# Queries in two halves of 50, 128-column score weights, and a planner that counts ScalarE's table: one change to a four-layer cross-attention kernel

## The chip, the cores and the metric

The kernel runs on one core of one Trainium2 chip. TensorE (PE for its matmuls, PEld for its weight loads), VectorE (DVE), ScalarE (ACT), GpSimd (POOL) and SyncE (SP, which issues the DMAs) run side by side, each through its own list of instructions, in that list's order; they wait for one another on semaphores. The metric is device time in microseconds of one launch; lower is better.

## The reference

The input is a batch of 16 with 100 query rows of 256 numbers (`x`), and a context of 361 rows of 256 numbers (`ctx_1024`) with a mask over the 361 keys. Everything is fp32. Four cross-attention layers follow each other, each with 16 heads:

```
L0: LayerNorm(x), LayerNorm(ctx); Q,K,V with biases, head size 16; softmax(QK^T/4) V; Wo, residual;
    LayerNorm, w1 (256 -> 1024), exact GELU, w2 (1024 -> 256), residual
L1: RMSNorm(x); Q,K,V without biases, head size 64; softmax(QK^T) V; Wo, residual
L2: Q,K,V, head size 64; rotary embedding of Q and K; mask; softmax(QK^T/8) V; Wo, residual; LayerNorm
L3: LayerNorm(x), LayerNorm(ctx); Q,K,V with biases, head size 16; softmax(QK^T/4) V; Wo, residual
```

So for each of the 16 batch elements and each layer there are 16 score matrices of 100 x 361, which need a softmax, a transposition (TensorE contracts over partitions), and a product with V.

## The kernel before

**Work list and planner.** `tile_xattn_layers` does not issue instructions as it goes. Each step (`Plan.add`) is recorded as a piece of work: the engines that may do it with its estimated occupancy and latency in ns, the buffers it reads and writes, and, for TensorE, the array's mode. `Plan.order` then takes pieces one at a time: it looks at all whose inputs are done and whose buffers are free, estimates when each could start on its best engine, and takes the earliest. Ties go by rank. A rank is the batch's place times `ORDER["lag"]`, less the length of the chain of work behind the piece, plus a number of its own out of the long list `ORDER["place"]`. The result is one fixed list for each engine. Two batch elements are under way at a time, in buffers of parity `p = b % 2`, so that one's column work lies beside the other's softmax.

**TensorE's modes.** The 128 x 128 array is used in parts. `on_columns` (line 726) cuts the weights into 32 columns and runs four matmuls beside each other (mode `col32`; the projections, the products with V, the output projections and the feed-forward). Scores of head size 64 (line 832) and all transpositions run as two halves of 64 rows each (`row64`); scores of head size 16 run as four quarters of 32 rows (`row32`). The planner adds `Plan.CHANGE[mode]` when it goes from one mode to another, and `ORDER["keep"]`, `"run"` and `"pull"` hold it in a mode or draw it to one.

**One unit of attention** (`Attention.unit`, 4 heads; 4 units a layer, 256 in all): `scores` writes four PSUM banks, one a head, with the queries as weights (100 columns) and the keys moving in two parts of 181 and 180 columns. For each head `exponential` copies the scores out of PSUM negated with their maximum (DVE, line 885; with the mask lines 879 and 882) and takes the exponential with its sum on ACT (line 891). For each pair of heads `softmax` inverts the sums (DVE, line 855) and divides (POOL, line 862). `transposed` (line 926) turns the 100 x 384 probabilities into 3 x 128 x 100: a transposition loads 128 columns of probabilities as weights and moves the identity. The rows are cut at 64, so the two that run beside each other have 64 and 36 rows, and move 64 and 36 columns. Each pair's first 64 queries go to one PSUM bank and are copied to `pT` (384 columns); the last 36 of both pairs share a bank `rest`, copied once a unit (432 columns). `copied` (lines 607 ACT, 609 DVE) lets the planner choose the engine. `weighted` multiplies by V (line 726).

**Around it.** `inv_root` and `normalize` (lines 632 and 643, POOL) make the norms, `queries_T` (line 667) transposes normalized queries, and its copies are lines 607 and 609, or 687 and 689 where a scale and a shift go with it. `keys_T` (754) transposes the context, `rows_of` (709) transposes back. `rotated` (781 to 793) applies the rotary embedding. `feed_forward` computes GELU in 8 ACT instructions (line 1257). Exponential and GELU are in different tables of ScalarE, so the program has a table load ahead of the first exponential after a GELU and ahead of each GELU block. The planner before has that load only in the estimate of the GELU piece (`8 * 245.0 + 2560`); the load itself stands in the program where the next exponential is.

**Start.** SP's queue issues the context, `x`, the column vectors `crow`, and the weight slabs in that order. The second context transfer waits for a memset of `ctxr` on POOL.

Of the kernel before, what the change touches and what calls it, by code (L numbers as in the profile page):

```python
# [26 lines left out]
SCORE_BANKS = 5  # L27

# [3 lines left out]
for _name, _w in (  # L32
# [23 lines left out]
    "lag": 262500, "pull": 1.05, "window": 0,  # L56
    "keep": {None: 4710, "row64": 360, "row32": 180, "col64": 5940, "col32": 2180},
    "run": {None: 0, "row64": 28190, "row32": 38220, "col64": 62800, "col32": 390},
    "batch": (-548000, -33500, 0, 0, 0, 0, 0, 0, 0, 0, 0, 0, 0, 0, 14000, -395500),
    "place": [  # L60
        100 * k for k in (
        1776, 1453, -142, -1201, -1962, -875, -1272, -1989, 482, -1959, -1129, -88, -4927,
        -3879, -2673, -19, -2982, 335, 200, -5963, -3867, -2489, -3290, -3547, -1559, -3672,
        602, 1581, -1237, -596, -892, -2024, -2482, -2746, -3675, -6084, -4418, -2962, -2419,
        -2347, -1399, -1767, -676, -4804, -3312, -4682, -3996, -950, -4319, -2634, 152, -4596,
        -4245, -4636, -3397, -2411, -4617, -1436, 1812, 478, -590, -3084, -3225, -157, -347,
        -1306, -36, -182, 2463, 2269, 2471, -1236, -226, -48, -2453, -824, -689, -240, -1480,
        -391, -171, 371, -1768, -2183, -2349, -2481, 1673, -1111, 32, 25, 1577, -514, -23,
        -1722, 3615, 62, -2886, -1417, -3429, -5371, -2487, -917, 340, -2084, 948, 1034, -1280,
        376, -1062, -727, 190, -606, 1116, -1324, -1597, -131, -943, 1382, 2231, 2480, -3400,  # L70
        -748, -2254, -1153, -2683, -2519, -1789, -5353, -2696, -2986, -2331, -2031, -4065,
        -3099, -2421, -171, -2559, 1016, -6786, -2846, -2199, -1555, -157, -1767, -1656, -3138,
        -1222, 2168, -631, -524, -4580, -574, 597, -514, -1139, 1487, 1898, -982, -233, 477,
        2044, -522, -2119, -3681, -1016, -671, 2120, 3576, 2286, -266, 3381, 723, 247, 1826,
        774, 948, -3623, -2236, 984, -2841, 310, 61, 2466, -3684, -6034, 1564, 1183, -2853, 537,
        -1192, -2567, -1296, 108, -3693, 149, -718, -1842, 780, 685, 1596, 3206, 156, 3888,
        1907, 2379, 1212, 1530, -3100, 2948, 1039, -288, -1177, -1310, -2820, -3017, 433, 151,
        -39, 1813, -33, 2599, -2329, -1178, -1118, 1344, -1750, -3151, -1387, -3185, -3845,
        -8129, -7410, -4599, -3978, -4283, -3026, -4766, -6536, -4866, -4851, -8579, -4112,
        -6439, -1860, -481, -2093, -540, -2396, -4045, -1076, -2195, -70, 1766, 165, -176,  # L80
        -1338, -918, -12, 1834, 2889, 1336, -1772, 1062, -3022, 2129, 611, 1207, -2448, -6678,
        -981, -133, 380, -1319, -722, -558, 2201, 2070, 640, 1748, 2253, 4103, 5971, 5712, 4011,
        3044, 722, 5181, 4108, 5603, 2863, 3615, 4070, 3505, 4100, 1973, 2673, 3145, 3356, 3367,
        5844, 3350, 2666, 6351, 2740, 5441, 3794, 495, 3120, 2070, -601, -856, -2641, 335,
        -2107, -3659, -1701, 378, 778, 1172, -739, 1007, 542, -108, -2248, 2953, -1482, -932,
        3100, -1364, 1555, 3374, 238, 3536, 4315, 3827, 4485, 3600, 2067, -880, 4682, 3885,
        3987, 5494, 4942, 6102, 3437, 4869, 1221, 3493, 1237, 2378, 1389, 266, 2904, 2874, 2176,
        936, -826, -1283, -1678, 654, -2718, -7, 4162, -524, -774, 511, -684, 3038, -1031, 2912,
        3195, 2452, 575, 493, 2016, 1582, 1498, -1241, -2078, -1407, -3506, -2378, -1649, -3375,
        -3472, -878, -594, -94, -2271, -2722, -2086, -5299, -6556, -4953, -2896, -463, -5380,  # L90
        -2620, -2181, -2583, -1142, 273, -2589, -3385, 987, 2285, 484, 765, -386, 3057, 1070,
        1200, 292, 763, 26, -5488, -2236, 259, -6763, -2594, -4453, -4645, -7113, -8246, -5633,
        -8943, -5849, -8851, -9101, -6157, -3672, -4940, -4203, -6547, -7698, -5075, -2078,
        -1789, -4219, -2670, -227, 100, 3388, 4070, 1516, -104, 2126, -432, 2456, 2021, 4097,
        2055, 2009, 6506, -667, -54, -1179, -34, 3966, 2359, -414, 1217, 3474, 2676, -1197, 857,
        1108, 4961, 1038, -3603, -260, 94, -1383, -960, 4578, 3569, 4863, 3041, 4067, 3943, 559,
        629, 1048, -963, 504, 79, -56, 734, 1352, 375, 1930, -2827, 1022, -297, 1587, 3516,
        -1027, -845, 1898, -1616, -1197, 384, 2016, 3496, 4418, 2467, 2775, 3097, 3600, 2898,
        3321, 435, -99, -1056, 4084, 2305, 1957, 2885, 1769, 3160, 1712, -4221, -1615, -1270,
        708, 999, -245, 44, 3282, 2595, 5822, 2335, 3929, 2251, 3141, -1056, -1690, -851, 1712,  # L100
        -289, 1963, 4576, 4722, 1801, -432, 1256, -1161, 1210, -3366, -1607, -3406, -2015, 1592,
        -266, -2447, -512, -1015, -345, -469, -4154,
# [19 lines left out]
class Work:  # L122
    __slots__ = (
        "engines", "fn", "bufs", "takes", "next", "then", "n_after", "ready", "tail", "batch",
        "mode", "modes", "index", "start", "end", "engine", "place", "rank",
# [25 lines left out]
class Plan:  # L151

    CHANGE = {"row64": 170, "row32": 191, "col32": 141, None: 190}
# [18 lines left out]
    def add(self, engines, fn, reads=(), writes=(), takes=(), mode=None, begun=()):  # L172
# [3 lines left out]
        w.engines, w.fn, w.batch = engines, fn, self.batch  # L176
# [36 lines left out]
    def order(self):  # L213
# [11 lines left out]
        mode, run = None, 0.0  # L225
# [5 lines left out]
        while len(done) < len(self.work):  # L231
            held, able, at_hand = set(), [], {}
            for _, i in ready:
# [23 lines left out]
                for e, occ, lat in w.engines:  # L257
                    s = max(t, free_at[e])
                    if e == "PE" and not set_now:
                        lat = lat + self.CHANGE[w.modes[0]]  # L260
                    if cost is None or s + lat < cost - 1:
                        engine, cost, start, busy = e, s + lat, s, occ
# [15 lines left out]
            if e == "PE":  # L278
                run = run + occ if set_now else occ
                if not set_now:  # L280
                    mode = w.modes[0]
                    occ += self.CHANGE[mode]
                w.mode = mode
            else:
                w.mode = e
            free_at[e] = start + occ
# [24 lines left out]
def tile_xattn_layers(  # L311
# [18 lines left out]
    def slots_of(name, n, shape, dtype=F32, pool=const):  # L330
# [16 lines left out]
        "two": slots_of("two", 32, [P, 2]),  # L347
        "mv": slots_of("mv", 8, [P, NKC, 8]),
    }
    for p in range(2):  # L350
# [5 lines left out]
        slots[f"qT{p}"] = slots_of(f"qT{p}", 1, [P, 8, S])  # L356
# [11 lines left out]
    for t in slots["prob"]:  # L368
        nc.gpsimd.memset(t[:S, SK:], 0.0)
# [71 lines left out]
    crow = const.tile([NCOLS, P], F32, name="crow")  # L441
# [5 lines left out]
    crow_b = load_const(crow, colvecs, 0.1, "crow")  # L447
# [26 lines left out]

    colt = const.tile([P, NCOLS], F32, name="colt")
# [3 lines left out]
    def transpose_cols(_):  # L479
        nc.tensor.transpose(cps.ap[:, :NCOLS], crow, ident[:NCOLS, :NCOLS])  # L480
# [4 lines left out]
    plan.add(on_pe((NCOLS, 1)), transpose_cols, reads=[crow_b], writes=[cps])  # L485
# [155 lines left out]
    def normalize(mv, dst, src, dst_f, src_f, j, n):  # L641
# [6 lines left out]
        plan.add(on_pool(395), fn, reads=[mv, src], writes=[dst])  # L648
# [121 lines left out]
    def rotated(ps, n, cos, sin, dst, dst_f, rep, rot, name):  # L770
# [3 lines left out]
        def shaped(a):  # L774
            return a.rearrange("p (r s) -> p r s", r=rep) if rep > 1 else a

        def wide(a):
            return a.unsqueeze(1).to_broadcast([P, rep, n // rep]) if rep > 1 else a
# [4 lines left out]
        def times_sin(_):  # L783
            a = shaped(sw.ap[:, :n])
            nc.gpsimd.tensor_tensor(a, a, wide(sin()), ALU.mult)  # L785

        def times_cos(_):
            nc.vector.tensor_tensor(
                shaped(dst_f(dst.ap)), shaped(ps.ap[:, :n]), wide(cos()), ALU.mult
            )  # L790

        def both(_):
            nc.gpsimd.tensor_tensor(dst_f(dst.ap), dst_f(dst.ap), sw.ap[:, :n], ALU.add)  # L793
# [6 lines left out]
    class Attention:  # L800
# [17 lines left out]
        def unit(self, i):  # L818
# [9 lines left out]
            def scores(_):  # L828
                for g in groups:
                    for k0, k1 in ((0, half), (half, SK)):  # L830
                        for h in g:
                            nc.tensor.matmul(  # L832
                                banks[h].ap[:S, k0:k1], lhsT=self.q_of(h),
# [15 lines left out]
        def softmax(self, banks, shares, pair, name, probs):  # L849
            sums, rsum = (plan.buf("two", f"{k}_{name}") for k in ("sum", "rsum"))  # L850
            for j, h in enumerate(pair):
                self.exponential(banks[h], shares[h], sums, j, h, probs)

            def inverse(_):
                nc.vector.reciprocal(rsum.ap[:S], sums.ap[:S])  # L855

            plan.add(on_dve(2), inverse, reads=[sums], writes=[rsum])
            for j, h in enumerate(pair):
                p = probs[h]

                def divide(_, j=j, p=p):
                    nc.gpsimd.tensor_scalar(  # L862
                        p.ap[:S, :SK], p.ap[:S, :SK], rsum.ap[:S, j : j + 1], 1.0,
# [5 lines left out]
        def exponential(self, bank, share, sums, j, h, probs):  # L869

            neg_max = plan.buf("two", f"mx_{self.name}_{h}")
            prob = probs[h] = plan.buf("prob", f"prob_{self.name}_{h}")
            masked = self.cap is not None

            def p():
                return prob.ap[:S, :SK]
# [516 lines left out]
```

## Time and profile before

| | |
|---|---|
| Time, median of 3 runs | 1972.56 us (1968.7 to 1972.88) |
| The profiled execution | 1968.26 us, of which the span is 1966.5 us |
| Granted TensorE clock, mean | 0.995 |
| Busy: PE / PEld | 1924.7 us / 1269.7 us |
| Busy: DVE / ACT / POOL | 1276.4 us / 1196.7 us / 1042.4 us |
| Transpositions of probabilities, line 926 | 6144 loads, 6144 matmuls |
| Scores, line 832 | 4096 loads, 4096 matmuls (two for each in the program) |
| Copies to `pT` | 540 on ACT, 228 on DVE |
| Table loads on ACT | 33, of 1283 ns each |

A group's mean is the time from dispatch to the modelled end of one instruction, and matmuls overlap, so the pace of TensorE is not read from means but from when instructions of a run start. A line such as `1028.18 0.58 PE L926 MATMUL ... x12` in the timeline says that 12 matmuls of line 926 began at 1028.18 us and the last ended 0.58 us later; `[0.59 <-POOL prob L862]` says that the engine sat idle for 0.59 us and what ended that. In the list of waits the three numbers are the total in us, how often, and the longest.

### The profile page before, as it was taken

The numbers are of one execution on the slowest core, as the hardware profiler recorded it, in microseconds if no ns is written. First come the engines' busy times: TensorE is split into PE (matmuls) and PEld (weight loads), VectorE is DVE, ScalarE is ACT, GpSimd is POOL, SyncE is SP. The second block draws the span as 40 slices with busy tenths as digits, with TensorE's granted clock in tenths as the row PEclk, the third lists the DMA queues.
The fourth block names the chain that finished last, engine by engine and source line by source line (L and its number), as shares of the span: only waits on it lengthen the run. The fifth ranks groups of instructions, "written<-read, shape, count | busy, mean of one in ns | idle before, by whom it ended". The sixth has DMA issues, their size and how long they took to land.

```text
span 1966.5 us, 99772 instructions
## 1 busy us (share of the span) xinstructions
PE 1924.7 (98%) x43881; PEld 1269.7 (65%) x43881; DVE 1276.4 (65%) x4452; ACT 1196.7 (61%) x3470; POOL 1042.4 (53%) x1680
## 2 busy tenths in 40 slices
PE   8999999999999999999999999999999999999997
PEld 4667666666666666666666666666656666665666
DVE  4556667766576665766657676566766657765576
ACT  4656656665566656666556565665666556665546
POOL 5354645545455564655546555464654545554464
PEclk9999999999999999999999999999999999999998
DMA  7000000000000000000000000000000000000000
GB/s 300 3 3 14 5 12 8 3 14 5 12 7 3 14 6 14 5 5 12 5 14 6 11 8 3 14 5 12 7 3 14 5 12 8 3 14 5 3 3 7
DMA packets 14731, 29.95 MB, mean 15 GB/s; under 512 B 3362, under 2 KB 12376, under 8 KB 12888
## 3 DMA queue, kind: packets, MB, share of 16 engines
q1 hardware_dynamic: 14296, 23.56, 3.8%
q8 instruction: 345, 5.65, 1.2%
q14 instruction: 90, 0.74, 0.1%
HBM read 21.92 MB, written 1.64 MB: 12 GB/s over the span
## 4 chain that ended last, share of the span: by engine, by line
PE 89%; POOL 3%; ACT 3%; DVE 2%; issue 1%; DMA 1%; SPq 0%; DVEq 0%; POOLq 0%; ACTq 0%
PE ps L726 64%; PE ps L832 14%; PE ps L926 10%; ACT prob L891 1%; POOL prob L862 1%; DVE prob L885 1%; PE ps L667 1%; ACT L891 1%; DVE pT L609 1%; POOL kT L793 1%; POOL sw L785 0%; DMA slab<-slabs_dram 0%; PE ps L754 0%; DMA mask<-mask_dram 0%; PE ps L709 0%
## 5 line engine op out<-in xcount | busy, mean ns | idle before, releaser
L862 POOL TENSOR_SCALAR prob<-prob,two 100x361 f32<-100x361 f32 x1024 | 568.2, 570 | 478.1 <-DVE two L855 390.1
L891 ACT ACTIVATE prob<-prob,two 100x361 f32<-100x361 f32 x1024 | 604.8, 595 | 141.1 <-DVE prob L885 101.4
L885 DVE TENSOR_SCALAR_CACHE_REDUCE prob<-ps 100x361 f32<-100x361 f32 x768 | 375.1, 528 | 79.2 <-PE ps L832 61.5
L726 PE MATMUL ps<-slab,cT 128*32 128x512 f32 (+1 forms) x3072 | 360.8, 595 | 0.0
L726 PE MATMUL ps<-cT,slab 128*32 128x361 f32 x4096 | 348.1, 469 | 2.5 <-DVE prob L885 1.8
L832 PE MATMUL ps<-kT,qT 32*100 32x181 f32 (+3 forms) x4096 | 301.1, 327 | 0.4 <-ACT oT L607 0.4
L607 ACT COPY pT<-ps 128x384 f32<-128x384 f32 (+1 forms) x540 | 236.7, 494 | 68.3 <-PE ps L926 65.2
L832 PEld LDWEIGHTS ps<-kT,qT 32*100 32x100 f32 (+1 forms) x4096 | 228.1, 163 | 72.6 <-issue 35.5
L926 PEld LDWEIGHTS ps<-ident,prob 64*128 64x128 f32 (+1 forms) x6144 | 218.4, 140 | 86.4 <-POOL prob L862 50.8
L926 PE MATMUL ps<-ident,prob 64*128 64x64 f32 (+1 forms) x6144 | 245.7, 228 | 5.0 <-issue 2.2
L609 DVE COPY pT<-ps 128x432 f32<-128x432 f32 (+1 forms) x228 | 126.0, 578 | 130.0 <-PE ps L926 129.4
L726 PEld LDWEIGHTS ps<-cT,slab 128*32 128x32 f32 x4096 | 121.9, 109 | 132.5 <-issue 114.6
L891 ACT ACTIVATION_READ_ACCUMULATOR prob<-prob,two 100x1 f32 x1024 | 196.0, 191 | 0.0
L726 PEld LDWEIGHTS ps<-slab,cT 128*32 128x32 f32 (+1 forms) x3072 | 88.5, 108 | 145.9 <-issue 136.6
L607 ACT COPY v<-ps 128x512 f32<-128x512 f32 (+1 forms) x136 | 79.3, 583 | 165.3 <-PE ps L726 165.3
L785 POOL TENSOR_TENSOR sw<-sw,rot 128x361 f32<-128x361 f32 x128 | 105.5, 824 | 125.2 <-DVE two L855 71.4
L726 PE MATMUL ps<-pT,v 128*32 128x100 f32 (+1 forms) x6144 | 158.5, 250 | 2.7 <-issue 1.7
L726 PEld LDWEIGHTS ps<-pT,v 128*32 128x32 f32 (+1 forms) x6144 | 137.2, 110 | 31.5 <-issue 17.5
L879 DVE TENSOR_TENSOR prob<-ps,cap 100x361 f32<-100x361 f32 x256 | 126.5, 525 | 31.9 <-PE ps L832 27.1
L855 DVE RECIPROCAL two<-two 100x2 f32<-100x2 f32 x512 | 81.5, 160 | 94.3 <-ACT prob L891 92.7
L726 PE MATMUL ps<-xT,slab 128*32 128x100 f32 x5120 | 124.4, 251 | 15.3 <-ACT xT L607 13.7
L726 PEld LDWEIGHTS ps<-xT,slab 128*32 128x32 f32 x5120 | 112.7, 110 | 34.1 <-ACT xT L607 23.7
(105 smaller groups left out, 2380.4 us busy)
## 6 DMA issues: line engine op xcount, KB each, us to landing
slab<-slabs_dram SPq DMA_DIRECT2D x11, 1024.0 KB
ctxr<-ctx_dram SPq DMA_DIRECT2D x16, 256.0 KB
ctxr<-ctx_dram SPq DMA_DIRECT2D x16, 105.0 KB
x<-x_dram SPq DMA_DIRECT2D x16, 100.0 KB
out_dram<-x SPq DMA_DIRECT2D x16, 100.0 KB
slab<-slabs_dram SPq DMA_DIRECT2D x2, 512.0 KB
mask<-mask_dram SPq DMA_DIRECT2D x16, 45.1 KB
rows<-rowvecs_dram SPq DMA_DIRECT2D x1, 640.0 KB
```

Source lines behind the costliest of these rows:

```text
L607: nc.scalar.copy(dst(), src())
L609: nc.vector.tensor_copy(dst(), src())
L667: nc.tensor.transpose(tp(i)[:, c, :], src.ap[q0:q1, c * P : (c + 1) * P], ident[q0:q1, q0:q1])
L726: nc.tensor.matmul(out_f(at + t, at + t1), lhsT=lhsT[:, t:t1], rhs=rhs, start=start, stop=stop, tile_position=(0, at + t),)
L785: nc.gpsimd.tensor_tensor(a, a, wide(sin()), ALU.mult)
L832: nc.tensor.matmul(banks[h].ap[:S, k0:k1], lhsT=self.q_of(h), rhs=self.k_of(h)[:, k0:k1], start=(k0 == 0), stop=(k1 == SK), skip_group_che ...
L855: nc.vector.reciprocal(rsum.ap[:S], sums.ap[:S])
L862: nc.gpsimd.tensor_scalar(p.ap[:S, :SK], p.ap[:S, :SK], rsum.ap[:S, j : j + 1], 1.0, ALU.mult, ALU.mult,)
L879: nc.vector.tensor_tensor(p(), bank.ap[:S, :SK], self.cap.ap[:S, :], ALU.min)
L885: nc.vector.tensor_scalar(p(), bank.ap[:S, :SK], -1.0, None, ALU.mult, ALU.min, accum_out=neg_max.ap[:S, 0:1],)
L891: nc.scalar.activation(p(), p(), AF.Exp, bias=neg_max.ap[:S, 0:1], scale=1.0 if masked else -1.0, accum_out=sums.ap[:S, j : j + 1],)
L926: nc.tensor.transpose(out[:, c, :], probs[h].ap[q0:q1, c * KP : (c + 1) * KP], ident[q0:q1, q0:q1],)
```

## The change

- Queries are cut into two halves of 50, and each half's rows start at a multiple of 64: rows 0 to 49 and 64 to 113. The queries of both parities now lie in two constant tiles `wide_q`, [128, 7 * 114 + 128], zeroed at the start, in which each head's or pair's block is 114 columns wide (`QP = 64 + 50`) with 14 unused columns between its halves.
- The scores' weights are the 128 columns from a block's start, so scores, softmax and division run on 128 partitions; the 28 extra rows are not used. Moving data stay 181 and 180 columns.
- `transposed` moves 50 columns in both halves; each pair has its own two PSUM banks, and four copies of 300 columns a unit take the place of two of 384 and one of 432.
- The planner keeps the loaded ACT table (`table`) and adds 1283 ns to an exponential or GELU that needs the other one. Its estimates change: 48 ns for a step of transpositions (61.7 before), `CHANGE` 143 for `row64` (170) and 140 for `col32` (141), the exponential 580 ns (538), `normalize` 520 (395), `scaled` 450 (395), `make_rot` 2270 (2120), the negation by 73 ns less, GELU 1850.
- All ranks and the numbers of `ORDER` are new. Of the small buffers there are 28 `two` (32), and the column vectors land in an `sw` buffer in place of a tile of their own.

The diff, cut to its core (the list of ranks left out):

```diff
+QH = 50
+QP = 64 + QH
+T_STEP = 48.0
...
-    "lag": 262500, "pull": 1.05, "window": 0,
-    "keep": {None: 4710, "row64": 360, "row32": 180, "col64": 5940, "col32": 2180},
-    "run": {None: 0, "row64": 28190, "row32": 38220, "col64": 62800, "col32": 390},
+    "lag": 218600, "pull": 3.1, "window": 0,
+    "keep": {None: 5670, "row64": 190, "row32": 770, "col64": 5360, "col32": 2780},
+    "run": {None: 0, "row64": 31110, "row32": 41350, "col64": 68880, "col32": 0},
...
-    CHANGE = {"row64": 170, "row32": 191, "col32": 141, None: 190}
+    CHANGE = {"row64": 143, "row32": 191, "col32": 140, None: 190}
+    TABLE = 1283
...
+                    if e == "ACT" and w.table not in (None, table):
+                        lat = lat + self.TABLE
...
+                if e == "ACT" and w.table not in (None, table):
+                    table = w.table
+                    occ += self.TABLE
...
-        "two": slots_of("two", 32, [P, 2]),
+        "two": slots_of("two", 28, [P, 2]),
...
-        slots[f"qT{p}"] = slots_of(f"qT{p}", 1, [P, 8, S])
+        wide_q[p] = const.tile([P, 7 * QP + P], F32, name=f"qT{p}")
+        nc.gpsimd.memset(wide_q[p], 0.0)
+        a = wide_q[p][:, :]
+        slots[f"qT{p}"] = [
+            bass.AP(tensor=a.tensor, offset=a.offset, ap=[a.ap[0], [QP, 8], [64, 2], [1, QH]])
+        ]
...
+    def halves(a):
+        return a.rearrange("p (m i s) -> p m i s", i=2, s=QH)
...
-                                banks[h].ap[:S, k0:k1], lhsT=self.q_of(h),
+                                banks[h].ap[:, k0:k1], lhsT=self.q_of(h),
...
             plan.add(
-                [("ACT", 538.0, 660.0)], exp, reads=[prob, neg_max], writes=[prob, sums]
+                [("ACT", 580.0, 690.0)], exp, reads=[prob, neg_max], writes=[prob, sums], table="exp"
             )
...
             for u, pair in enumerate(pairs):
-                first = plan.buf("ps", f"{name}_tp{u}")
+                banks = [plan.buf("ps", f"{name}_tp{u}{i}") for i in range(2)]
...
+                            for i in range(2):
+                                r = slice(64 * i, 64 * i + QH)
                                 nc.tensor.transpose(
-                                    out[:, c, :], probs[h].ap[q0:q1, c * KP : (c + 1) * KP],
-                                    ident[q0:q1, q0:q1],
+                                    tp(i)[:, j, c, :], probs[h].ap[r, c * KP : (c + 1) * KP],
+                                    ident[r, r],
                                 )
...
-                    on_pe((64, 6), least=61.7), fn,
+                    on_pe((QH, 6), least=T_STEP), fn,
...
+                for i in range(2):
+                    copied(
+                        lambda u=u, i=i: pT.ap[
+                            :KP, 2 * u : 2 * u + 2, :, i * QH : (i + 1) * QH
+                        ],
+                        lambda i=i, tp=tp: tp(i), 2 * NKC * QH, [banks[i]], [pT],
+                    )
...
         def q_of(h):
             r0 = (h % 2) * 64
-            return qT.ap[r0 : r0 + 64, h // 2, :]
+            c0 = h // 2 * QP
+            return wide_q[p][r0 : r0 + 64, c0 : c0 + P]
...
-            [("ACT", 8 * 245.0 + 2560, 8 * 245.0 + 1400)], gelu, reads=[*pss, colt_b],
-            writes=[hT],
+            [("ACT", 1850.0, 1990.0)], gelu, reads=[*pss, colt_b], writes=[hT], table="gelu"
```

## The prediction

> **What bounds the kernel now.** I read the page first: which engine is full, and who is on the chain that ended last.
>
> ```profile
> span 1966.5 us, 99772 instructions
> ...
> PE 1924.7 (98%) x43881; PEld 1269.7 (65%) x43881; DVE 1276.4 (65%) x4452; ACT 1196.7 (61%) x3470; POOL 1042.4 (53%) x1680
> ...
> PE 89%; POOL 3%; ACT 3%; DVE 2%; issue 1%; DMA 1%; SPq 0%; DVEq 0%; POOLq 0%; ACTq 0%
> ...
> L832 PEld LDWEIGHTS ps<-kT,qT 32*100 32x100 f32 (+1 forms) x4096 | 228.1, 163 | 72.6 <-issue 35.5
> L926 PEld LDWEIGHTS ps<-ident,prob 64*128 64x128 f32 (+1 forms) x6144 | 218.4, 140 | 86.4 <-POOL prob L862 50.8
> L926 PE MATMUL ps<-ident,prob 64*128 64x64 f32 (+1 forms) x6144 | 245.7, 228 | 5.0 <-issue 2.2
> ```
>
> TensorE is the bound: 98% busy and 89% of the chain, the others at 53 to 65%. So I count what TensorE is spared or given, and treat work elsewhere as covered unless PE waits for it. Next the timeline, for the pace inside a run of transpositions and the price of a change of mode; three stretches:
>
> ```profile
> 903.15 0.20 PEld L667 LDWEIGHTS ps<-ident,z 64*128 64x128 f32 x4 [0.59 <-issue]
> ...
> 928.49 0.96 PE L926 MATMUL ps<-ident,prob 64*128 64x64 f32 x24
> 929.38 1.42 PE L726 MATMUL ps<-cT,slab 128*32 128x361 f32 x16
> ...
> 1028.18 0.58 PE L926 MATMUL ps<-ident,prob 64*128 64x64 f32 x12
> 1028.70 1.07 PE L726 MATMUL ps<-slab,zT 128*32 128x256 f32 x16
> ```
>
> A run of 24 transpositions (12 steps of two halves) ends in column work after 0.89 us, one of 12 (6 steps) after 0.52. The difference is 6 steps, 62 ns each by the unrounded records, and what is left, 143 ns, is the run's fixed part. Then the waits of PE and one place where the longest recurring one happens:
>
> ```profile
> PE ps L726 <- ACT xT L607: 13.7, 11, 1.2
> ```
>
> ```profile
> 999.29 1.28 ACT L891 ACT_TABLE_LOAD   x1
> 1000.59 0.60 ACT L891 ACTIVATE prob<-prob,two 100x361 f32<-100x361 f32 x1
> ...
> 1001.18 0.58 ACT L891 ACTIVATE prob<-prob,two 100x361 f32<-100x361 f32 x1
> ...
> 1001.76 0.24 ACT L607 COPY xT<-ps 128x128 f32<-128x128 f32 x1
> ...
> 1002.06 2.95 PE L726 MATMUL ps<-xT,slab 128*32 128x100 f32 x128 [1.25 <-ACT xT L607]
> ```
>
> In 11 of 16 batch elements a table load and two exponentials stand on ACT ahead of the copy that PE needs next.
>
> **The change, part by part.**
>
> *The pace of transpositions (a).* There are 3072 steps on line 926. A step moved 64 columns, now 50; but it still loads 128 columns of weights. Which of the two sets 62 ns? In the records, the first two loads of a run start 57 to 58 ns apart (the four loads of line 667 above; 58 in runs of line 926 too), before any matmul streams; later ones 62. With 100 columns (line 709) the first two are 44 apart. So a load takes about 0.44 ns a column, and 128 columns cannot follow each other faster than about 57; the smallest distance among 5631 on line 926 is 56. Line 512 agrees: loads of 128 columns with one moving column still come 111 ns apart. Moving 64 columns adds about 4. I take 58: 3072 x 4 = -12.3 us. Bounds: 62 as now (0), and 62 x 50/64 = 48.4, if the pace went with the moved columns (-41.8).
>
> One rule of the Trainium skill speaks against this part. "TensorE: Matmul & The Clock Gate", section "LDWEIGHTS (loading the stationary operand)", has the load's time follow the columns alone, rows being free, at columns / 1.2, so 107 ns for 128. The trace's 57 contradicts that rate for transpositions, but agrees that nothing but the column count matters (halves of 36 and 64 rows both load in 140). By the rule as it stands the pace would not move, and the sum below would be +2 instead of -10.
>
> *The ends of those runs (b).* The last step streams 14 columns fewer, 12 ns at 0.83 ns a column (361 columns take 303), but a run also has one interval fewer than steps, so it gives 4 back: 8 ns over the 318 runs that end in another mode, -2.6 us. Bounds 0 and -4.
>
> *Score weights (c).* 256 score blocks. Within one, a step of 181 columns takes 153 ns, longer than any load here, so only the first load shows. Loads of 32 columns take 110 ns (line 726), of 100 take 163 (line 832): 0.78 a column, 28 more columns 22 ns, 256 x 22 = +5.6 us. The row of 128 columns in line 926 is shorter (140), so -5.9 is the other bound; it is a transposition, so I take the score rows.
>
> *Changes of mode (d).* From the two programs' lists of instructions I counted changes between column work, 64-row and 32-row work: 843 before, 955 after; column work to transpositions 216 to 281 and back 248 to 298, the other kinds between -8 and +7. Prices are medians from the records (time from a run's first matmul to the next run's, less steps at pace): 151 ns into transpositions, 142 back, 191 out of 32-row scores, 145 into them. 65 x 151 + 50 x 142 is 16.9, the other kinds make -0.5: +16.4 us, all on the bound engine. At 90 and 190 ns a change it is 10 to 21.
>
> *ACT's table (e).* Still 33 loads. In the new list the exponential's load stands directly behind the GELU block in 15 of 16 elements (in the old list in two), and the copies of `xT` come later with no load between. I let the 11 waits go, 13.7 us, and half of three later ones of 1.0 to 1.2 us that follow them by 6 us: -15. Bounds 0 (the wait moves) and -17. What is late next there is the division on POOL, for which PEld waits 50.8 us in 79 pieces, mostly under running matmuls.
>
> *The start (f).* Two memsets of 926 columns stand ahead of the memset of `ctxr`. One of 1152 takes 1.03 us (line 373), so 0.83 each; SP's queue waits there, and behind it stand `x`, the column vectors and all weight slabs: +1.7 us (bounds 0 and 1.7).
>
> *Copies and the rest (g).* 768 copies to `pT` become 1024: by 0.83 and 1.04 ns a column 635 on ACT at 0.41 and 389 on DVE at 0.46 us, 439 us where there were 378. Both engines have over 600 us idle; PE waits for these copies 3.7 us now. Cost 0; without that cover a third more of that wait, +1.2. The 28 extra partitions cost nothing on DVE, ACT and POOL: the 128-partition row L1307 on POOL takes 492 ns, the 100-partition division 570. The strided query writes and fewer `two` buffers I cost at nothing, hidden likewise.
>
> *The new order otherwise (h).* PE's other waits over 0.3 us away from both ends make about 8 us. The estimates now stand nearer to the rows (exponentials follow each other by 0.58 us; estimate 538, now 580), and PE will be later than the planner believes (58 against 48 a step), which gives others time. I take half, -4; bounds -8 and +8.
>
> Sum: -12.3 - 2.6 + 5.6 + 16.4 - 15 + 1.7 + 0 - 4 = -10.2 us. The profiled execution took 1968.26 (span 1966.5 and 1.8 around it), so 1958; the median of the runs lies 4.3 above that, and from 1972.56 it is 1962.
>
> **The rivals.**
>
> *The pace follows the moved columns* (48.4 ns): (a) is -41.8, the sum -40, 1933. For it: in 64-row runs both readings give nearly the same pace now (64 columns at 0.83 is 53, the load 54 to 57), so the matmul could be what is seen. Against: the first interval of a run. Chance 0.10.
>
> *The loads keep 62 ns*: (a) is 0, the sum +2, 1975. For it: both halves load at once, and the extra 4 may come from that. Break-even is at 61. Chance 0.20.
>
> *The table wait moves instead of going*, and it ends slower. The place: ACT right behind GELU. The reload of 1.28 us and up to four exponentials of 0.58 now come ahead of copies out of PSUM. If PE has less than about 3.6 us of other work queued there, it waits, and (e) is 0: the sum +5, 1977; with a pace of 62 as well, +17, 1989. For it: 32 of 33 loads are still in the middle of a softmax. Against: the planner now counts them. Chance 0.20, of which 0.08 with 62.
>
> What is left, 0.50, is the forecast.
>
> **How the numbers follow.** A measurement of this kernel tells about 0.2% from no change, 4 us. The forecast's own spread (h, d) is some 9 us, so about 0.87 of it is faster by more than that; of the 62 ns case 0.2, of the moved wait at 58 ns a little, of the fast rival all: 0.58 faster. Within 0.2% lie a tenth of the forecast and half of the 62 ns case, with part of the moved wait: 0.19. Slower: 0.23. The range 1938 to 1982 leaves out the whole of the fast rival and the case in which both the pace stays and the wait moves.
>
> **What would show it.** In the changed profile: runs of 12 transpositions taking about 0.48 us to the next run and loads 57 to 59 ns apart (a); loads on the scores' line near 185 ns with the block's steps still at 153 (c); 955 changes of mode at the old prices (d); no recurring wait of PE for `xT` on ACT (e); PE's first matmul near 7 us instead of 5.5 (f). Loads under 54 ns apart, or a recurring wait of PE behind the exponential's table load, would make the prediction wrong.

## The result, and the profile after

The changed kernel takes 1979.95 us (median of 5 runs, 1979.52 to 1982.64) beside 1968.7 for the kernel before (5 runs, 1965.82 to 1972.88): a ratio of 1.0057, 95% interval 1.0039 to 1.0076. It is slower by 11 us, where the forecast was 10 faster; 1980 lies inside the range. The profiled execution, the slowest of the five, took 1982.64, its span 1980.7.

The page of the changed kernel. Its lines have moved: transpositions of probabilities are line 947 (926 before), scores 856 (832), column work 752 (726), copies 633 and 635 (607 and 609), the exponential 917, GELU 1279.

```profile
span 1980.7 us, 100200 instructions
...
PE 1948.9 (98%) x43881; PEld 1289.1 (65%) x43881; DVE 1333.6 (67%) x4661; ACT 1180.0 (60%) x3515; POOL 1043.2 (53%) x1684
...
PE 95%; DVE 1%; ACT 1%; DMA 1%; POOL 1%; issue 1%; SPq 0%; ACTq 0%; DVEq 0%; POOLq 0%
...
L947 PEld LDWEIGHTS ps<-ident,prob 50*128 50x128 f32 x6144 | 223.6, 140 | 129.6 <-issue 60.6
L856 PEld LDWEIGHTS ps<-kT,qT 32*128 32x128 f32 (+1 forms) x4096 | 241.5, 188 | 77.0 <-issue 32.7
```

TensorE now makes 95% of the chain (89% before): the waits on other engines did shrink, and TensorE's own time grew. A load for transpositions still takes 140 ns, and one for scores 188 instead of 163. Now the timeline of PE, a run of 12 transpositions and one of 24:

```profile
959.77 0.58 PE L947 MATMUL ps<-ident,prob 50*128 50x50 f32 x12
960.28 1.92 PE L752 MATMUL ps<-slab,cT 128*32 128x512 f32 x16
...
986.27 0.95 PE L947 MATMUL ps<-ident,prob 50*128 50x50 f32 x24
987.16 1.42 PE L752 MATMUL ps<-cT,slab 128*32 128x361 f32 x16
```

The next work begins 0.51 and 0.89 us after a run begins, as in the kernel before (0.52 and 0.89). From the unrounded records the medians are 506 and 878 ns: six steps take 372, so a step is 62.0 ns still, with 50 moved columns as with 64. Then what PE waited for:

```profile
PE ps L506 <- DMA sw<-colvecs_dram: 6.8, 1, 6.8
PE ps L947 <- POOL prob L888: 3.5, 6, 2.0
...
PE ps L947 <- ACT pT L633: 2.5, 14, 0.2
...
PE ps L752 <- DVE pT L635: 0.9, 2, 0.7
```

The recurring wait for `xT` on ACT is gone. On ACT the exponential's table load now stands directly behind the GELU block:

```profile
990.94 1.28 ACT L1279 ACT_TABLE_LOAD   x1
992.23 1.99 ACT L1279 ACTIVATE qT<-ps,colt 128x100 f32<-128x100 f32 x8
994.23 1.28 ACT L917 ACT_TABLE_LOAD   x1
995.53 0.60 ACT L917 ACTIVATE prob<-prob,two 128x361 f32<-128x361 f32 x1
```

So two of the three large terms are as forecast (955 changes of mode at 145 and 134 ns, the table wait gone), one is zero (the pace), and about 9 us more are missing. The experiments look for these.

### The profile page after: what moved, and what is told of

Same layout as the page of the kernel before. It is cut to its first block, busy times and chain, and to the rows that moved or that the text cites. A ratio compares the mean times of both kernels' runs of the same rounds, so it can differ in the third digit from the quotient of the medians.

```text
span 1980.7 us, 100200 instructions
## 1 busy us (share of the span) xinstructions
PE 1948.9 (98%) x43881; PEld 1289.1 (65%) x43881; DVE 1333.6 (67%) x4661; ACT 1180.0 (60%) x3515; POOL 1043.2 (53%) x1684
## 4 chain that ended last, share of the span: by engine, by line
PE 95%; DVE 1%; ACT 1%; DMA 1%; POOL 1%; issue 1%; SPq 0%; ACTq 0%; DVEq 0%; POOLq 0%
PE ps L752 69%; PE ps L856 14%; PE ps L947 11%; PE ps L693 1%; PE ps L780 1%; ACT pT L633 1%; DMA slab<-slabs_dram 1%; DVE prob L911 0%; ACT prob L917 0%; DMA mask<-mask_dram 0%; PE ps L735 0%; POOL prob L888 0%; DVE prob L905 0%; SPq L438 0%; DVE two L908 0%
## 5 line engine op out<-in xcount | busy, mean ns | idle before, releaser
L888 POOL TENSOR_SCALAR prob<-prob,two 128x361 f32<-128x361 f32 x1024 | 567.8, 571 | 470.0 <-DVE two L881 367.9
L917 ACT ACTIVATE prob<-prob,two 128x361 f32<-128x361 f32 x1024 | 603.5, 593 | 124.2 <-DVE prob L911 81.0
L911 DVE TENSOR_SCALAR_CACHE_REDUCE prob<-ps 128x361 f32<-128x361 f32 x768 | 375.4, 530 | 100.8 <-PE ps L947 56.4
L633 ACT COPY pT<-ps 128x300 f32<-128x300 f32 x635 | 238.2, 412 | 139.3 <-PE ps L947 121.4
L856 PE MATMUL ps<-kT,qT 32*128 32x181 f32 (+3 forms) x4096 | 308.5, 333 | 0.5 <-ACT pT L633 0.5
L947 PEld LDWEIGHTS ps<-ident,prob 50*128 50x128 f32 x6144 | 223.6, 140 | 129.6 <-issue 60.6
L856 PEld LDWEIGHTS ps<-kT,qT 32*128 32x128 f32 (+1 forms) x4096 | 241.5, 188 | 77.0 <-issue 32.7
L947 PE MATMUL ps<-ident,prob 50*128 50x50 f32 x6144 | 259.8, 227 | 6.6 <-POOL prob L888 3.5
L635 DVE COPY pT<-ps 128x300 f32<-128x300 f32 x389 | 172.8, 464 | 126.7 <-PE ps L947 124.4
L917 ACT ACTIVATION_READ_ACCUMULATOR prob<-prob,two 128x1 f32 x1024 | 194.8, 190 | 0.0
```

Source lines behind the costliest of these rows:

```text
L633: nc.scalar.copy(dst(), src())
L635: nc.vector.tensor_copy(dst(), src())
L856: nc.tensor.matmul(banks[h].ap[:, k0:k1], lhsT=self.q_of(h), rhs=self.k_of(h)[:, k0:k1], start=(k0 == 0), stop=(k1 == SK), skip_group_chec ...
L888: nc.gpsimd.tensor_scalar(p.ap[:, :SK], p.ap[:, :SK], rsum.ap[:, j : j + 1], 1.0, ALU.mult, ALU.mult,)
L911: nc.vector.tensor_scalar(p(), bank.ap[:, :SK], -1.0, None, ALU.mult, ALU.min, accum_out=neg_max.ap[:, 0:1],)
L917: nc.scalar.activation(p(), p(), AF.Exp, bias=neg_max.ap[:, 0:1], scale=1.0 if masked else -1.0, accum_out=sums.ap[:, j : j + 1],)
```

## The experiments

They take an order as given: the planner's loop gets a written list of pieces and engines in place of its search, so that one thing can be changed with all else in place. On each chip the kernel before was run beside them; its medians lay between 1968.7 and 1971.7, so kernels of different calls are compared by their ratios, 0.001 of which is 2 us.

```
-            for _, i in ready:
+            for i, on in SEQ[len(done) : len(done) + 1]:
                 w = self.work[i]
```

### The pace of transpositions

**e3_load_64.**

```
-    tp(i)[:, j, c, :], probs[h].ap[r, c * KP : (c + 1) * KP],
+    tp(i)[:64, j, c, :], probs[h].ap[r, c * KP : c * KP + 64],
```

> The changed kernel, but every transposition of probabilities loads only 64 of its 128 columns (half of the transposed probabilities is left out); 50 columns still move. Load theory: a load of 64 columns takes about 28 ns, so the 50 moved columns take over with 42 to 50 ns a step: runs of 12 near 420 ns instead of 506, and 35 to 60 us less than 1980. Issue theory: 62 ns, 506 and 1980 as before.

One run: 1939.63 us. Runs of 12 take 386 ns and runs of 24 take 651: a step is 44.2 ns, which is 50 columns at 0.84 (361 columns take 303 ns) and 2.2 ns over. PEld in this run (busy us and mean ns, then the idle time before):

```profile
L1258 PEld LDWEIGHTS ps<-ident,prob 50*64 50x64 f32 x6144 | 164.4, 109 | 137.9 <-issue 55.9 <-POOL prob L1199 40.3 <-POOL kT L1126 11.2
```

So it was the 128-column load that held 62 ns. With the load out of the way, 44.2 fits the moved columns as the next limit, but no run with 64-column loads varied them. By that reading 64 moved columns would ask for 53.7 + 2.2 = 56 ns, an estimate, which is less than the load's 62; so cutting them to 50 gave nothing.

**e2_third_load_105.** The third block has only 105 keys, so its load needs no 128 columns.

```
-    tp(i)[:, j, c, :], probs[h].ap[r, c * KP : (c + 1) * KP],
+    tp(i)[: KC[c], j, c, :], probs[h].ap[r, c * KP : c * KP + KC[c]],
```

> The changed kernel, but the third of a head's three transpositions loads its 105 real columns and not 128 with zeros; everything else is the same, order too. Load theory (the weight load's columns set the pace of a step, 62 ns for 128): a third of the 3072 steps load 23 columns fewer, 10 ns at 0.44, so -10 us against the changed kernel, about 1970, and pure runs of 12 transpositions from 506 to about 486 ns. Issue theory (62 ns is what four instructions cost, whatever they load or move): 1980, runs of 12 still at 506.

2012.12 us (2011.12 to 2014.55), ratio 1.0211, interval 1.0196 to 1.0227: neither. Fewer columns cost 30 us. By form:

```profile
L1258 PEld LDWEIGHTS ps<-ident,prob 50*128 50x128 f32 x4096 | 223.1, 156 | 128.8 <-issue 59.2 <-POOL prob L1199 36.6 <-POOL kT L1126 11.2
L1258 PEld LDWEIGHTS ps<-ident,prob 50*105 50x105 f32 x2048 | 196.4, 188 | 0.0
```

A load of 105 columns takes 188 ns, one of 128 takes 140 elsewhere (156 here on the mean, those behind a load of 105 included). Runs of 12 and 24 take 566 and 1001 ns, six steps 435. With 62 for the 128-column steps that leaves 93 ns for a step of 105. Either a change of width costs, or 105 is a bad width.

**e5_loads_121** cuts the keys 121, 120, 120, with all loads 121 wide. This and e10 have the kernel before's layout, in the order of e4 (below, 1952 us).

```
-KC = (KP, KP, SK - 2 * KP)
+KN, KO, KW = (121, 120, 120), (0, 121, 241), 121
-    probs[h].ap[q0:q1, c * KP : (c + 1) * KP]
+    probs[h].ap[q0:q1, KO[c] : KO[c] + KW]
```

> The kernel before in its order, the copy of xT moved up as in e4_xT_copy_first, and the 361 keys cut 121, 120, 120 instead of 128, 128, 105 for the transposed probabilities and the values, so that every load of these transpositions is 121 columns wide (nothing is left out). Load theory (a step takes its load's columns, as 128 columns take 62 ns and 64 no longer show): 62 x 121 / 128 = 58.6 ns, 3072 x 3.4 = 10.4 us less than e4_xT_copy_first: 1942, runs of 12 near 0.49 us. Rival (only loads of 128 columns are quick, as the loads of 105 columns in e2_third_load_105 suggest, which cost 30 ns a step): every step near 92 ns, 3072 x 30 = 92 us more: 2044.

2078.83 us (2075.33 to 2084.16), ratio 1.0562 (1.054 to 1.0583), some 130 us more than e4. The rival held, and more: 773 and 1408 ns, a step of 106 ns.

```profile
L1231 PEld LDWEIGHTS ps<-ident,prob 64*121 64x121 f32 (+1 forms) x6144 | 351.7, 184 | 83.6 <-issue 54.5 <-POOL prob L1167 21.3 <-POOL mv L937 6.1
```

All widths are equal here, so it isn't the change of width. 105 and 121 are odd; 64 and 128 are not. Hence the next one.

**e10_loads_122.**

```
+KN, KO, KW = (120, 120, 121), (0, 120, 240), 122
```

> The kernel of e4_xT_copy_first with the keys cut 120, 120, 121 and every load of the transposed probabilities 122 columns wide, from columns 0, 120 and 240 (nothing is left out). Theory of even widths (128, 100 and 64 columns loaded at about 0.44 to 0.48 ns a column, 105 and 121 at 0.87): 62 x 122 / 128 = 59.1 ns a step, 3072 x 2.9 = 9 us less than e4_xT_copy_first: 1943, runs of 24 2.9 x 12 = 35 ns shorter. Rival (only multiples of 4, or of 32, are quick, or an odd width was not what slowed 121): steps of 106 ns as in e5_loads_121, near 2079.

1945.9 us (1945.44 to 1948.0), ratio 0.9884 (0.9867 to 0.9902), with nothing left out. That is 0.002 under e4, 4 us where 9 were expected, and the two intervals overlap. But one more column than in e5 makes 133 us:

```profile
L1231 PEld LDWEIGHTS ps<-ident,prob 64*122 64x122 f32 (+1 forms) x6144 | 210.6, 137 | 85.8 <-POOL prob L1167 54.8 <-issue 22.1 <-POOL mv L937 6.1
```

Runs of 12 and 24 take 494 and 852 ns: a step is 59.6, and 2.4 ns on 3072 steps are 7 us. (e5 had odd starts as well as an odd width; in e2 only the width was odd, 105 from column 256.)

**e11_third_load_106 and e12_loads_100** return to the changed kernel. e11 is e2 with one column more (`KW = (KP, KP, 106)`), e12 is e3 with 100 in place of 64.

> The changed kernel in its own order, the third of a row's three loads 106 columns wide, not 128 (nothing is left out; the 106th column holds zeros). Theory of even widths: e2_third_load_105 was slow since 105 is odd. From 62 ns at 128 and 60 at 122 columns, 0.33 ns a column: 54.7 ns for a third of the 3072 steps, 7.5 us less than the changed kernel: 1972, runs of 12 near 0.49 us. Rival (two widths in turn cost a wait, whatever they are): as e2_third_load_105, runs of 12 at 0.57 us, 2012.

1974.1 us (1969.9 to 1976.34), ratio 1.0015 (1.0005 to 1.0025): 8 us less than the changed kernel, 38 less than e2. Runs of 12 and 24 take 486 and 842 ns, six steps 356; with 62 for the steps of 128, a step of 106 takes 54.

> The changed kernel in its own order, every load of the transposed probabilities 100 columns wide (the probabilities of 28 keys in the first two chunks, and of 5 in the third, are left out). If a step goes down by 0.33 ns a column, as from 128 to 122: 52.7 ns a step, a run of 24 takes 316 ns more than a run of 12, 1951. If it is in proportion to the columns: 48.4 ns, 290, 1938. Below 44 ns the 50 moved columns would hold it, as in e3_load_64.

One run: 1955.56 us; runs of 12 and 24 take 430 and 732 ns, a step 50.3, between the two. The time is above both forecasts (1951 and 1938). Together:

| columns loaded | moved | a step, ns | ns a loaded column |
|---|---|---|---|
| 128 (both kernels) | 64, 50 | 62.0 | 0.48 |
| 122 (e10) | 64 | 59.6 | 0.49 |
| 106 (e11) | 50 | 54 | 0.51 |
| 100 (e12) | 50 | 50.3 | 0.50 |
| 64 (e3) | 50 | 44.2 | no longer set by the load |
| 121 (e5) | 64 | 106 | 0.88 |
| 105 (e2) | 50 | 93 | 0.89 |

### The layout and the order

**e4_xT_copy_first** takes only the table wait away from the kernel before: in its own written order, one piece moves.

```
 SEQ:  copy 1 of L1's xT
+      copy 2 of L1's xT
       (table load) exponential, exponential
-      copy 2 of L1's xT
```

> The kernel before in its own order, with one kind of piece moved: the second copy of L1's xT comes directly behind the first, ahead of the exponential's table load and two exponentials. Table theory (11 waits of 1.25 us are PE's loss and nothing takes their place): -13.7 us, 1955. Rival (exponentials come later by a copy of 0.25 us, but the division and transpositions that follow were just in time, so the wait only moves behind them): 1966 to 1969, no recurring wait for xT but a new one of about 1 us on line 926 or its twin.

1952.16 us (1949.97 to 1953.47), ratio 0.9904 (0.9889 to 0.9919): 19 us less, where the waits themselves were 13.7. (The two profiled executions differ by 14.8, near to the waits; the rest may be other small waits or spread.) On ACT both copies now stand ahead of the load:

```profile
994.47 0.39 ACT L909 COPY xT<-ps 128x72 f32<-128x72 f32 x2 [1.85 <-PE ps L969]
994.87 1.28 ACT L1193 ACT_TABLE_LOAD   x1
996.17 0.60 ACT L1193 ACTIVATE prob<-prob,two 100x361 f32<-100x361 f32 x1
```

**e1_layout_old_order** is the other half: the new layout in the old order, with its 843 changes.

> The new layout (halves of 50, score weights of 128 columns, two banks and two copies a pair) with the old order of all pieces: each engine takes its pieces in the sequence of the kernel before; only the third and fourth copy of a unit are new, put beside the copies they replace. 843 changes of mode, as before. Order theory (the 112 more changes of mode make the changed kernel slow, the layout costs little): first loads of score blocks +5.8 us, ends of transposition runs -2.9, start +1.2: 4 us over the kernel before, 1973, and 7 under the changed one. Layout theory (the layout itself, its copies and 128-partition softmax, makes it slow and the order is neutral): 11 us over before, 1980.

1999.26 us (1997.19 to 2001.01), ratio 1.0147 (1.013 to 1.0164): neither theory; 0.009, or 18 us, slower than the changed kernel. PE's waits had a new kind (3.7 us for `pT` in the kernel before):

```profile
PE ps L1062 <- ACT xT L943: 14.0, 11, 1.5
PE ps L1062 <- ACT pT L943: 8.2, 35, 1.0
...
PE ps L1062 <- DVE pT L945: 4.0, 15, 0.9
```

**e6_layout_xT_first** is e1 with the move of e4.

> The new layout in the order of before, as e1_layout_old_order, with L1's second copy of xT put directly behind the first, ahead of the exponential's table load. If the new order is worth what this one move is worth: 1999.3 - 19.5 = 1980, as the changed kernel; then the order's 112 further changes of mode (16 us) have bought nothing but the waits behind the copies of the transposed probabilities, and the two cancel. If the new order is worth more than the move, this run stays above 1985; if its changes of mode cost more than they hide, it falls below 1975.

1977.23 us (1975.91 to 1979.01), ratio 1.0044 (1.0029 to 1.0059), 20 us less than e1. The intervals of e6 and of the changed kernel (1.0039 to 1.0076) overlap. So beyond this one move, the new order with its 112 further changes of mode gains nothing that these runs can tell, in the new layout. But in this layout it also removes a cost, of which e6 still has all: 45 runs of 24 between 32-row scores and column work take 1128 ns, where e4 has 887.

**e7_copies_on_two_engines** asks whether two copies behind each other on one engine are that cost. In e6 this is so for 218 of the 512 pairs.

```
 SEQ:  copy of a pair's first half on ACT (or DVE)
-      copy of its second half on the same engine
+      copy of its second half on DVE (or ACT)
```

> As e6_layout_xT_first, with the second copy of each pair's transposed probabilities on the other of ACT and DVE than the first. If PE waits there because two copies of a pair stand one behind the other on one engine (waits of PE for pT of 12.2 us in e1_layout_old_order, 3.7 in the kernel before), half of the difference goes: 4 us of the waits over 0.3 us and about as much of the shorter ones: 1972. Rival (the other engine is busy at that moment with exponentials or negations, and it is the count of copies that costs): no change, 1980, or slower.

1987.28 us (1985.97 to 1991.91), ratio 1.0099 (1.0082 to 1.0115): 11 us slower than e6, nearest to the rival. The runs of 24 stay at 1128 ns, PE's waits for `pT` at 12.6 us (12.2 in e6), and DVE has 55 us more to do, 1352 us where e6 has 1297. Giving the second copy an engine of its own shortens nothing that PE waits for.

**e9_four_banks** then asks about the banks, with the old halves of 64 and 36, old widths and e4's order.

```
-            rest = plan.buf("ps", f"{name}_tp_rest")
             for u, pair in enumerate(pairs):
                 first = plan.buf("ps", f"{name}_tp{u}")
+                rest = plan.buf("ps", f"{name}_tp{u}_rest")
```

> The kernel of e4_xT_copy_first (the old halves of 64 and 36, score weights 100 wide), with the bank for the rests of both pairs divided in two, one for each pair, each with its own copy (4 x 3 x 36 = 432 columns become 2 x 216): a unit's transpositions now take four PSUM banks and four copies, as in the new layout, in e6_layout_xT_first's order; nothing else is changed. Bank theory (column work behind a run of 24 gets the bank that the first copy frees, because a fourth one is taken): the 45 and 37 runs of 24 that end in column work take 1.13 and 1.07 us instead of 0.89 and 0.83, excess of transpositions to columns 63 instead of 48 us, 1952 + 15 = 1967. Rival (the 50 and 50 halves or the wide scores cause it): runs stay at 0.89 and 0.83, 1952.

1975.74 us (1972.58 to 1977.27), ratio 1.003 (1.002 to 1.004): 25 us more than e4, more than the 15 expected, and the runs of 24 are longer as foretold: 1207 and 1152 ns, where e4 has 887 and 831. The same stretch of the same order, e4 first:

```profile
907.63 0.96 PE L1228 MATMUL ps<-ident,prob 64*128 64x64 f32 x24
908.52 1.92 PE L1028 MATMUL ps<-slab,cT 128*32 128x512 f32 x16
...
912.22 0.96 PE L1228 MATMUL ps<-ident,prob 64*128 64x64 f32 x24
913.10 1.42 PE L1028 MATMUL ps<-cT,slab 128*32 128x361 f32 x16
```

```profile
915.89 0.96 PE L1237 MATMUL ps<-ident,prob 64*128 64x64 f32 x24
917.29 1.92 PE L1037 MATMUL ps<-slab,cT 128*32 128x512 f32 x16 [0.43 <-ACT pT L918]
...
920.98 0.96 PE L1237 MATMUL ps<-ident,prob 64*128 64x64 f32 x24
922.19 1.42 PE L1037 MATMUL ps<-cT,slab 128*32 128x361 f32 x16 [0.25 <-ACT pT L918]
```

In e4 the column work starts 0.89 us after the run; in e9 1.40 and 1.21, when a copy to `pT` has ended. That work reads nothing of `pT`: it projects keys and values of the context. It waits for the bank it writes. The kernel has eight banks (`ps`) to give out. By the programs' lists, column work that directly follows a unit's second pair gets a bank of that unit's first pair in 17 of 165 places in e4; in e9 and in e6 in 94 of 165, in the changed kernel in 45 of 132. There the bank is free only when the pair's copy has ended. Waits of PE in e9:

```profile
PE ps L1037 <- ACT pT L918: 22.0, 75, 1.0
```

The fourth copy and the fourth bank came together, but places within one kernel tell them apart. After runs of 24 in e9, column work begins 0.47 us (median) after the last transposition in the 78 places where it gets a bank of the first pair, and 0.15 us in the 68 where it gets another, though all of them have four copies. Beyond 0.15 us a place, the 78 make 26.0 us, about the whole of what e9 lost to e4. In e6 the same sum is 18.6 us (76 places), in the changed kernel 2.8 us (14 places). Where other work stands between a unit's two pairs, column work gets such a bank in 31 further places of the changed kernel and begins after 0.15 us (median) all the same.

### The scores' weights and the start

**e8_scores_114_start.**

```
-            return wide_q[p][r0 : r0 + 64, c0 : c0 + P]
+            return wide_q[p][r0 : r0 + 64, c0 : c0 + QP]
...
-        nc.gpsimd.memset(wide_q[p], 0.0)      # ahead of vs and ctxr
+        nc.gpsimd.memset(wide_q[p], 0.0)      # behind them
```

> The changed kernel in its own order, with score weights 114 columns wide instead of 128, and the memsets of the two query tiles moved behind those that SP's queue waits for. By my sum: 256 x 14 x 0.78 ns = 2.8 us less for the loads (near 175 ns instead of 188, the excess of 32-row scores 11 ns less) and 1.2 us less at the start (first matmul at 5.5 us): 1976. Rival (widths other than 128 are slower, as in e2_third_load_105): 256 x 40 ns = 10 us more, 1989.

1977.28 us (1972.84 to 1979.96), ratio 1.0038 (1.0025 to 1.005): the right way by 0.0019, but its interval overlaps that of the changed kernel, so the time alone doesn't show it. The records do: the time past the last step of 32-row scores is 202.5 ns (214 with 128 columns, 190 with 100), and PE's first matmul starts at 5.43 us (6.77 in the changed kernel).

```profile
L1167 PEld LDWEIGHTS ps<-kT,qT 32*114 32x114 f32 (+1 forms) x4096 | 235.1, 176 | 77.1 <-issue 32.7 <-DVE prob L1222 17.4 <-DVE two L1192 11.1
```

## Why the prediction was wrong, step by step

The ratios make a ladder between the two kernels, in parts of 1970 us: the table wait taken away -18.9 (e4, 0.9904); four banks, in the old order, +24.8 (e9, 1.003); the rest of the layout +2.8 (e6, 1.0044); the rest of the order +2.6 (1.0057). Together +11.2. The last two are each within about one interval of nothing.

**(a) The pace, -12.3 forecast, 0 measured: the step that failed.** I read the load's own pace from the first two loads of a run (57 to 58 ns apart), gave the other 4 ns to the moved columns, and wrote "I take 58". Those 4 ns do not go with the moved columns: a step takes 62 at 128 loaded columns with 64 and with 50 moved. The rival that ends at 1975, "the loads keep 62 ns", is what happened to the pace, and it names break-even at 61. The first interval of a run is not the pace of loads in sequence, which is 62; what makes the 4 ns between them stays open. The rows that the sum read did not hold the load and the moved columns apart; one run with 64-column loads did.

**(g) The copies, 0 forecast: the other step that failed.** Copies as such were rightly costed at nothing: ACT and DVE do have room. What was missed is that a fourth copy means a fourth bank, held from PE's first transposition to the copy's end, with work of PE queued behind it on the same eight banks. In the old order this is +25 us (e9). The changed kernel's own waits for such banks are short (2.8 us), but its order has 112 more changes of mode.

**(d) Changes of mode, +16.4: the count and the prices held.** 955 changes; 145 and 134 ns where 151 and 142 were taken (the 8 less at runs' ends is term b). What they buy can be read beside e6 and e9: runs of 24 are split by column work, so that copies end under it. 63 runs of 24 that end in column work are left of 144, and 14 places where PE waits for a bank just used, of 76. That the changes buy this is argued from these counts; no run took the changes alone away. The sum took them as a cost for nothing and left the banks out. In the changed kernel the banks and the order beyond the table wait come to 24.8 + 2.6 = 27.4 us, where (d), (g) and (h) together had 12.4. At the prices, 16.4 of it are changes; 2.8 are the waits for banks just named, and 2.5 are transpositions that waited for a copy to `pT` (line 947 in the waits above). Some 6 us were not traced to a cause.

**(e) The table wait, -15: right, and low.** -18.9 by e4's ratio, 14.8 by its profile. That exponentials would come ahead of other copies and make PE wait, the third rival, did not happen.

**(b), (c), (f): right.** -2.6, +5.6 and +1.7 make +4.7; the rest of the layout measured +2.8. That is no clean test of their sum, since the waits for banks fall in the same step, from 26.0 us in e9 to 18.6 in e6. But each shows in its place: a run's fixed part went from 143 to 134 ns, a score load from 163 to 188, the first matmul from 5.52 to 6.77 us.

**(h) Other waits, -4: not there.** The order's rest is +2.6, or nothing.

The account, which closes by its making since the ladder's steps are parts of one difference: (a) is short by 12.3, (d), (g) and (h) by 15.0; (e) is better by 3.9, and (b), (c) and (f) by 1.9. That is 21.5 us, and the forecast missed by 21.4 (from -10.2 to +11.2).

**The rule of the skill.** The page "TensorE: Matmul & The Clock Gate" of the Trainium skill, section "LDWEIGHTS (loading the stationary operand)", has loads take columns / 1.2 ns, and by it the pace would not have moved, which was the right answer. But even widths of these transpositions went almost twice as fast, 62 for 128 where it says 107, and the measurements decide. The rule's figure comes near to three other rows. One is the odd widths: 88 and 101 ns for 105 and 121 columns, where 93 and 106 were measured. The second is line 512, whose loads of 128 columns are not transpositions: they come 111 ns apart, which the prediction took as agreeing with its 57, though it is twice that. The third is the kernel before at 50.87 us, where the granted clock was 0.50: there the 128-column transposition loads of line 754 took 107 ns a step, and 62 at 23.34 us, where it was 1.00. (Steps of 107 also stand at 6 and 14 us, ahead of the profile's first record of the clock at 16.6 us.)

```profile
48.21 1.86 PEld L512 LDWEIGHTS ps<-colt,slab 128*128 128x128 f32 x16 [0.85 <-issue]
...
core 0: us, PE busy (x) PEld busy (x) DVE busy (x) POOL busy (x), PEclk, DMA share, GB/s
23.34:23.79 0.45, 0.44 (x12) 0.45 (x12) 0.00 (x0) 0.00 (x0) 1.00 1.07 419
50.87:51.63 0.76, 0.70 (x12) 0.76 (x12) 0.00 (x0) 0.00 (x0) 0.50 0.00 0
```

The prediction's remark that nothing but the column count matters does not hold either: 105 columns cost more than 128.

## What to carry to other kernels

When two things could set a pace, cut each down separately on the chip before costing an edit: here a run with 64-column loads, in which a step fell from 62 to 44 ns, tells that the loads held the pace. Count what an edit does to the number of buffers in flight, above all of PSUM banks, as well as to the engines' time: a copy that an idle engine does for nothing still holds a bank, and unrelated work of the bound engine can wait for it. And when a change brings a new layout and a new order together, run each part alone; here one moved copy was worth 19 us, and the version with it and 122-column loads (1945.9 us, ratio 0.9884) beats both kernels.

## What the runs showed of the hardware

Loads of the transposed probabilities with an odd number of columns are far slower than with an even one: a step of 121 takes 106 ns, one of 122 takes 59.6; 105 takes 93, 106 takes 54. The odd ones, at 0.88 and 0.89 ns a column, are near line 512, where loads of 128 columns that are not transpositions come 111 ns apart, 0.87 a column. The difference between odd and even is seen for these fp32 transpositions; whether other loads have it was not tried, and the scores' loads follow a line of their own (163, 176 and 188 ns at 100, 114 and 128 columns). Between 100 and 128 even columns a step costs 0.48 to 0.51 ns a loaded column; at 128 it is the same with 50 and with 64 moved. At a granted clock of 0.50 a step of 128 took 107 ns in place of 62 (line 754 in the kernel before).
